# A four-layer image kernel: one tile for the exponentials' ring and delta, two PSUM banks for values, and four smaller moves between engines

## The chip, the cores and the metric

The kernel runs on one core of one Trainium2 chip. The metric is the device time of one execution in microseconds (us). A NeuronCore has five engines that run side by side: TensorE (PE, matrix products; its weight loads are listed as PEld), VectorE (DVE), ScalarE (ACT), GpSimd (POOL), and SyncE (SP), whose queue issues nearly all transfers between the chip's main memory and the on-chip memory SBUF. PE writes into PSUM[...].

## The reference

The input x is four images of 128 channels and 64 x 64 pixels in float32. Four layers follow each other, each of the form x = x + layer(group_norm(x)), with 32 groups per image. Below, n is the number of pixels, 4096.

```python
x = x + L0(gn(x))    # attention over all 4096 pixels of an image
x = x + L1(gn(x))    # 5x5 convolution, weights assembled from tables
x = x + L2(gn(x))    # two selective scans (one forward, one over the flipped pixels)
x = x + L3(gn(x))    # 3x3 convolution

# L0
q, k, v = xt @ Wq.T + bq, xt @ Wk.T + bk, xt @ Wv.T + bv      # xt: n x 128
out = softmax(q @ k.T * 128 ** -0.5) @ v

# L2, for each half of the channels (64 channels, 64 states)
xc = silu(causal_conv4(u) + conv_b); xt = xc.T
delta = softplus(xt @ Wd + bd); Bm = xt @ WB; Cm = xt @ WC
dA = exp(delta[..., None] * A); dBx = (delta * xt)[..., None] * Bm[:, :, None, :]
h[t] = dA[t] * h[t-1] + dBx[t]                                 # along the pixels
y = sum_n(h * Cm) + D * xt
```

## The kernel before

**Two streams of instructions in one order.** The program is written out by Python generators. One generator, `scan_core`, yields the ticks of the scans of all images; another, `images`, yields everything else (attention, convolution, scan operands of the images in turn, then the back ends). The driver at the end of `program` alternates them: each half tick earns a credit of `PACE / 2` (1.4), or `ENDPACE / 2` (0.75) once the ticks of the last image begin, and the other stream's steps are drawn until the credit is spent; a step yields its cost, such as `PRODUCT` (0.86), `SLOT` (0.7) or `HOP` (1.7). Each engine then executes its own instructions in the order in which they were written out. Waits between engines come from the tiles: a tile taken from a pool under a tag whose buffer is in use waits until all accesses of the tile that had the buffer are over.

**The ticks.** An image has 256 ticks, 1024 in all. A tick is 1024 pixels for 128 pairs of channel and state: POOL forms `db` (L1183, 128 x 1024), ACT the decays `da` (L1176), DVE runs the recurrence (L1193), and the result `hc` is multiplied by the rows of C either on DVE (L1196, two of 128 x 512) or on POOL (L1214, one of 128 x 1024). `to_pool(i)` decides which, at the tick's recurrence, from i mod 5: residues 0, 2 and 4 go to POOL while the set `ready` holds "operands", residues 1 and 3 otherwise; for the last image it is i mod 3 equal to 2. PE sums `hc` over the states (`collect`, L1228). The ticks of image b may start once its first operands are ready; so they run beside the attention, convolution and operands of image b+1, and those of the last image stand alone with the back ends.

**Attention.** `attention_start` normalises x in quarters and computes the values v in eight groups of 512 pixels: `keys(i)` is four products into one bank (L399), `take(i)` their eviction by ACT (L404). For images 1 to 3 it runs interleaved with the operands of the image before (`both`). `attention` then walks 256 steps: 8 blocks of 512 queries by 32 key tiles of 128. A step u computes scores (L467) into bank s or s2, ACT takes their exponential into column block u mod 8 of a ring of 8 x 512 (L473), and two steps later `values` (L479) adds the product with v. The sums of the exponentials are made by PE (`sums`, L501, four tiles at a time) or, for image 0, on DVE and POOL (`side_sums`, L521). At the end of a block `evict` copies sums and products out by ACT (zs L527, raw L529), `turn` (L541) and `invert` (L550, L552) form the reciprocals, `widen_out` (L459) spreads them, and `settle` (L564, L565) adds the block to x. In the last block all of that stood after the last values.

**Operands of the scans.** `scan_prep` normalises the image into `xn` in four pieces of 1024 pixels and stores the image; `scan_operands` works through 8 groups of 512 pixels on a table of slots: group i starts in slot 5i with the taps of the causal convolution on PE (L984; one view of xn forward, one from its end backward), `halves` on ACT (xc L998, tanh L1003), `silu` (L1007), three products (L1016), the evictions of the rows of B and C (`row`, L1021), `softplus` and `exp` on ACT, `digits` on DVE (L1035, L1036). In groups, with a switch of ACT's table, `logs` takes logarithms (L1065), `join` (L1041) adds them to delta on POOL, `drives` (L1046) multiplies delta and xc on POOL; each chunk of 1024 is stored by SP after its join (`dd`) and its drive (`dxd`). For image 0 the logarithms come in three batches (slots 20, 40 and 50), for the others in two (slots 30 and 50); joins follow one slot later, drives two slots after the joins. `delta` and the ring of the exponentials are both 128 x 4096 and take turns in the buffer "xt":

```python
ring = pools["big"].tile([P, NRING, MM], F32, tag="xt", name=f"pt_{b}")      # attention
delta = pools["big"].tile([P, L], F32, tag="xt", name=f"delta_{b}")          # scan_operands
```

The order on each engine around the change is thus fixed by the slots, the costs that are yielded, and the driver's credits.

Of the kernel before, what the change touches and what calls it, by code (L numbers as in the profile page):

```python
# [52 lines left out]
def conv_preact_kernel(  # L53
# [233 lines left out]
    def large(n, name):  # L287
        return pools["big"].tile([P, ASIZE], F32, tag=f"A{n % 2}", name=name)
    NRING = 8

# [86 lines left out]
    def attention_start(b, xn):  # L377
# [16 lines left out]
        def keys(i):  # L394

            tag = "s" if b > 0 else "saz"[i % 3]
            pvs[i] = bank(tag, f"pv_{b}_{i}").rearrange("p (t c) -> p t c", c=C)
            for t in range(TPM):
                nc.tensor.matmul(  # L399
                    pvs[i][:, t, :], xn[:, bass.ts(i * TPM + t, P)], wv, start=True, stop=True  # L400
                )
# [20 lines left out]
    def attention(b, xs, xn, v, st, safe, loads):  # L422

        ring = pools["big"].tile([P, NRING, MM], F32, tag="xt", name=f"pt_{b}")
        later = {}
# [96 lines left out]

        def evict(blk):
            zs = None
            if not fill:
                zs = pools["bg"].tile([P, MM], F32, tag="zs", bufs=1, name=f"zs_{b}_{blk}")
                nc.scalar.copy(zs, zp.pop(blk))  # L527
            raw = pools["bg"].tile([P, MM], F32, tag="raw", bufs=1, name=f"raw_{b}_{blk}")
            nc.scalar.copy(raw, acc.pop(blk))  # L529
            state[blk] = raw, zs  # L530

# [41 lines left out]
        yield HOP  # L573
        for u in range(N + 2):
            blk, j = divmod(u, NJT)
            cost = sums_due(u)
            if u < N:
                if safe and j == 0:
                    row_max(blk)
                scores(u)  # L580
                cost += PRODUCT
            w = u - 2
            if 0 <= w < N:
                values(w)
                cost += PRODUCT
                d = w % NJT
                if fill:
                    side_sums(w)
                elif d == NJT - 1:
                    sums(w)  # L590
                    cost += PRODUCT
                elif d % 4 == 3:
                    due.append((w, u + (2 if d == 3 else 1), u + NRING - 5))
                if d == NJT - 1:
                    evict(blk - 1)
                    if blk < NM:
                        for n, f in ((1, turn), (2, invert), (4, widen_out), (5, settle)):
                            after(u, n, f, blk - 1)
                    else:
                        turn(blk - 1)  # L600
                        invert(blk - 1)
                        yield PRODUCT
                        widen_out(blk - 1)
                        settle(blk - 1)
                        ready.add((b, "attended"))
                        break
            if j == 17 and blk + 1 < NM:
# [5 lines left out]
            next(loads, None)  # L613
            yield cost or HOP


# [326 lines left out]
    def scan_prep(b, xs, st, mats4):  # L943
# [8 lines left out]

        def piece(i):
            cut = slice(i * L // 4, (i + 1) * L // 4)
            normalise(xn[:, pad + cut.start : pad + cut.stop], xs[:, cut], gn)
            nc.sync.dma_start(xsd[:, cut], xs[:, cut])

        piece(0)
        piece(3)
        yield HOP  # L960
        return scan_operands(b, xn, mats4, piece)

    def scan_operands(b, xn, mats4, piece):
# [6 lines left out]
        xc = large(b, f"xc_{b}")[:, :L]  # L970
        delta = pools["big"].tile([P, L], F32, tag="xt", name=f"delta_{b}")
        pts, ths, pzs, pbs, us = {}, {}, {}, {}, {}
# [22 lines left out]
        def halves(i):  # L995

            pt = pts.pop(i)
            nc.scalar.activation(xc[:, bass.ts(i, MM)], pt, AF.Identity, scale=0.5, bias=hbias)  # L998

# [19 lines left out]
        def row(i, m):  # L1019
            bs = pools["bg"].tile([P, MM], F32, tag="w", bufs=4, name=f"bs{m}_{b}_{i}")  # L1020
            nc.scalar.copy(bs, pbs.pop((i, m)))  # L1021
            c, h = divmod(i, CH // MM)
            nc.sync.dma_start(bc[m - 1][c][:, bass.ts(h, MM)], bs)
# [14 lines left out]
        def join(c):  # L1038
            for i in range(c * CH // MM, (c + 1) * CH // MM):
                cut = bass.ts(i, MM)  # L1040
                nc.gpsimd.tensor_tensor(delta[:, cut], delta[:, cut], us.pop(i), ALU.add)  # L1041
            nc.sync.dma_start(dd[c], delta[:, bass.ts(c, CH)])
# [51 lines left out]
        for i, j in zip(cuts, cuts[1:]):  # L1094
            t = EVERY * (j - 1) + 15
            at(t, logs, i, j)
            for n, c in enumerate(range(i // PER, j // PER)):
                at(t + 1 + n, join, c)
                at(t + 3 + n, drives, c)
                at(t + 4 + n, ready.add, (b, "operands", c))  # L1100
        at(1, piece, 1)
        at(2, piece, 2)
        at(2, ready.add, (b, "read"))
        at(EVERY * (NM - 1) + 4, ready.add, (b, "taps"))
        ready.add("operands")
        for t in range(max(slots) + 1):
            for f, args in slots.get(t, ()):
                f(*args)
            yield SLOT
        ready.discard("operands")  # L1110
        ready.add((b, "all"))

# [3 lines left out]
    def scan_core(mats4, ynds, before, widen, result):  # L1116
# [11 lines left out]
        def to_pool(i):  # L1128


            if i not in pooled:
                n = i % 5
                pooled[i] = (
                    i % 3 == 2 if ticks[i][0] + 1 == B
                    else n % 2 == 0 if "operands" in ready else n % 2 == 1
                )
# [163 lines left out]
    def program(safe):  # L1300
        nonlocal more
        mats4, ynds, ends = {}, {}, {}
        ready.clear()
        if safe:
            nc.sync.dma_start(cw[:, :NKEPT, :], kept)
# [257 lines left out]
```

## Time and profile before

| | us |
|---|---|
| median of 3 runs | 4474.22 (4471.26 to 4474.52) |
| the profiled execution's own time | 4477.01 |
| its span | 4475.2 |
| PE busy | 3978.4 |
| DVE busy | 3693.8 |
| POOL busy | 3661.3 |
| ACT busy | 2401.4 |

The span runs from the first to the last instruction of the profiled execution. A row of the groups, of the timeline or of the waits names line, engine, operation and output <- inputs; in a timeline the first two numbers are start and length, xN says how many instructions were merged, and a bracket gives the engine's idle time ahead of it with the instruction that ended it. PE's products in float32 appear as two MATMUL records each. The image stages in this execution are: attention 0 until 505 us, attention 1 from about 735 to 1385, attention 2 from 1686 to 2335, attention 3 from 2641 to 3287, each followed by a convolution and the operands; the ticks begin at 687 us.

### The profile page before, as it was taken

How to read it: one execution, taken by the hardware profiler on the slowest of the kernel's cores; microseconds unless marked ns; L12 is line 12 of the kernel's file. 1: busy time of each engine (PE TensorE's matmuls, PEld its weight loads, DVE VectorE, ACT ScalarE, POOL GpSimd, SP SyncE). 2: the span in 40 equal slices, each digit the busy share in tenths (PEclk: the TensorE clock that was granted, in tenths of full speed). 3: DMA queues.
4: the chain of work that ended last, by engine and by line, in shares of the span. 5: the costliest groups of instructions: out<-in, count | busy, mean ns of one | idle time of the engine just before them, and what ended most of it. 6: DMA issues, size and time to landing. Idle time of an engine off the chain costs nothing. (4 is left out here: it accounts for less than half of the span.)

```text
span 4475.2 us, 43573 instructions
## 1 busy us (share of the span) xinstructions
PE 3978.4 (89%) x13480; PEld 1478.5 (33%) x13480; DVE 3693.8 (83%) x3663; ACT 2401.4 (54%) x4424; POOL 3661.3 (82%) x1745
## 2 busy tenths in 40 slices
PE   8999997999999979999999979999999758576766
PEld 4444443333333323333333323333333212121212
DVE  4712217999998988999999879999999799999996
ACT  3333227666665476666664566666654754544442
POOL 3433307999998979999989889999999899999995
PEclk9999999999999989999999999999999868787888
DMA  1000016545454565455545655445545666656562
GB/s 63 9 1 1 5 47 232 179 162 177 172 176 155 184 214 207 172 176 172 180 147 176 204 215 180 171 168 173 181 151 182 216 232 205 230 196 230 179 235 78
DMA packets 210002, 719.86 MB, mean 161 GB/s; under 512 B 24800, under 2 KB 25696, under 8 KB 209632
## 3 DMA queue, kind: packets, MB, share of 16 engines
q1 hardware_dynamic: 208160, 716.26, 45.8%
q8 instruction: 108, 1.77, 0.2%
q14 instruction: 134, 1.10, 0.1%
q10 hardware_dynamic: 1600, 0.73, 0.1%
HBM read 649.07 MB, written 67.83 MB: 160 GB/s over the span
## 5 line engine op out<-in xcount | busy, mean ns | idle before, releaser
L1183 POOL TENSOR_TENSOR db<-dx,br 128x1024 f32<-128x1024 f32 x1024 | 2399.5, 2366 | 214.6 <-DMA dx<-dxd 55.9
L1176 ACT ACTIVATE da<-de,a_neg 128x512 f32<-128x512 f32 (+1 forms) x1795 | 1342.0, 751 | 740.5 <-DVE da L1193 449.5
L467 PE MATMUL sc<-r,x 128*128 128x512 f32 x2048 | 1080.8, 610 | 19.0 <-ACT r L436 12.4
L479 PE MATMUL acc<-pt,v 128*128 128x512 f32 x2048 | 1046.6, 593 | 1.7
L1214 POOL TENSOR_TENSOR hc<-hc,cr 128x1024 f32<-128x1024 f32 x406 | 959.7, 2364 | 17.3 <-ACT last L1209 15.5
L473 ACT ACTIVATE pt<-sc 128x512 f32<-128x512 f32 x1024 | 604.4, 590 | 571.9 <-PE sc L467 563.3
L1228 PE MATMUL y<-hc,sel 128*32 128x512 f32 x4096 | 657.1, 653 | 275.5 <-POOL hc L1214 264.2
L1196 DVE TENSOR_TENSOR hc<-da,cr 128x512 f32<-128x512 f32 (+1 forms) x1067 | 827.7, 776 | 68.5 <-issue 0.5
L1193 DVE TENSOR_TENSOR_SCAN da<-da,last,db 128x512 f32<-128x512 f32 (+1 forms) x464 | 728.0, 1569 | 23.6 <-POOL db L1183 17.5
L1193 DVE TENSOR_TENSOR_SCAN da<-da,da,db 128x512 f32<-128x512 f32 x449 | 577.9, 1287 | 12.7 <-ACT da L1176 12.1
L467 PEld LDWEIGHTS sc<-r,x 128*128 128x128 f32 x2048 | 358.7, 189 | 604.4 <-issue 377.3
L479 PEld LDWEIGHTS acc<-pt,v 128*128 128x128 f32 x2048 | 387.5, 190 | 497.2 <-issue 478.5
L1193 DVE TENSOR_TENSOR_SCAN hc<-da,last,db 128x512 f32<-128x512 f32 (+1 forms) x304 | 455.6, 1499 | 5.8 <-POOL db L1183 2.2
L1193 DVE TENSOR_TENSOR_SCAN hc<-da,hc,db 128x512 f32<-128x512 f32 x322 | 413.1, 1283 | 55.0 <-ACT da L1176 23.3
L521 POOL TENSOR_TENSOR sidep<-sidep,pt 128x512 f32<-128x512 f32 x120 | 170.5, 1421 | 280.0 <-ACT pt L473 277.8
L1228 PEld LDWEIGHTS y<-hc,sel 128*32 128x32 f32 x4096 | 94.4, 111 | 729.0 <-POOL hc L1214 355.2
L521 DVE TENSOR_TENSOR sided<-sided,pt 128x512 f32<-128x512 f32 x120 | 96.0, 800 | 227.5 <-ACT pt L473 226.1
L904 PE MATMUL pe<-df,cw 128*128 128x512 f32 x560 | 255.2, 598 | 0.0
L1193 DVE TENSOR_TENSOR_SCAN da<-da,db 128x512 f32<-128x512 f32 (+1 forms) x154 | 231.0, 1500 | 28.1 <-ACT da L1176 15.0
L646 PE MATMUL pcm<-xpm,cw 128*128 128x512 f32 x432 | 226.0, 666 | 24.5 <-ACT xpm L372 24.5
L501 PE MATMUL zp<-pt,ones 128*32 128x512 f32 x1536 | 203.6, 595 | 5.0 <-DVE xs L565 4.9
L1209 ACT COPY last<-da 128x1 f32<-128x1 f32 x469 | 73.1, 156 | 239.5 <-DVE hc L1196 237.8
(236 smaller groups left out, 2842.4 us busy)
## 6 DMA issues: line engine op xcount, KB each, us to landing
br<-bm SPq DMA_DIRECT2D x512, 512.0 KB, 5.2
cr<-cm SPq DMA_DIRECT2D x512, 512.0 KB, 4.0
de<-dd SPq DMA_DIRECT2D x64, 512.0 KB, 4.7
dx<-dxd SPq DMA_DIRECT2D x64, 512.0 KB, 6.3
x<-in_x_dram SPq DMA_DIRECT2D x16, 512.0 KB, 5.1
xs<-in_x_dram SPq DMA_DIRECT2D x16, 512.0 KB, 5.5
xsd<-xs SPq DMA_DIRECT2D x16, 512.0 KB, 5.3
xcd<-xc SPq DMA_DIRECT2D x16, 512.0 KB, 3.3
```

The source lines that it names most:

```text
L467: nc.tensor.matmul(sc, xn[:, bass.ts(j, P)], rq[blk], start=True, stop=True)
L473: nc.scalar.activation(pt, sc, AF.Exp)
L479: nc.tensor.matmul(acc[blk], v[:, j, :], ring[:, u % NRING, :], start=j == 0, stop=j == NJT - 1)
L521: eng.tensor_tensor(s, s, ring[:, u % NRING, :], ALU.add)
L646: nc.tensor.matmul(acc.rearrange("p (r w) -> p r w", w=W), weights[:, t, :], xp[:, y : y + RPM, dx : dx + W], start=t == 0, stop=t == k * ...
L904: nc.tensor.matmul(flat(acc), cw[:, w * K5 + dx, :] if w < HSUM else more[:, w - HSUM, dx, :], view(r, dx), start=k == 1, stop=k == total ...
L1176: nc.scalar.activation(da, rep["de", b, c, d, g][:, bass.ts(h, size)], AF.Exp, scale=a_neg[:, at(i)])
L1183: nc.gpsimd.tensor_tensor(dbs[i], rep["dx", b, c, d, g], rows["b", b, c, d, q], ALU.mult)
L1193: nc.vector.tensor_tensor_scan(h, da, db[:, cut], before, ALU.mult, ALU.add)
L1196: nc.vector.tensor_tensor(hc[:, cut], h, rows["c", b, c, d, q][:, cut], ALU.mult)
L1214: nc.gpsimd.tensor_tensor(hcs[i], hcs[i], rows["c", b, c, d, q], ALU.mult)
L1228: nc.tensor.matmul(y[r : r + SG, :], sel, hcs[i - KG + 1 + gg][:, bass.ts(h, MM)], start=q == 0, stop=False, tile_position=(0, r), skip_gr ...
```

## The change

Seven things change together. (1) `exchange` gives one tile to ring and delta of all images, in place of a new one each time. (2) For images 1 to 3 the values alternate between the banks s and s2 from group 3 on. (3) `join` of the second half of the chunks goes to DVE for images 1 to 3. (4) From the slot of the last C row until the operands' end, "drives" is in `ready`, and only residue 1 of the ticks goes to POOL. (5) The normalisation of the scans' input goes in pieces of 512, from both ends to the middle; the stores stay at 1024. (6) In the last block the last four values are held back: sums come ahead of them, and `turn`, `invert` and `widen_out` are placed among them. (7) For image 0 the first half of `halves` and the rows of C are written by DVE.

```diff
+    shared = {}
+    def exchange(b):
+        if b not in shared:
+            shared[b] = shared.get(b - 1)
+            if shared[b] is None:
+                shared[b] = pools["big"].tile([P, L], F32, tag="xt", name="exchange")
+        return shared[b]
...
-            tag = "s" if b > 0 else "saz"[i % 3]
+            tag = "saz"[i % 3] if b == 0 else "s" if i < 3 else ("s", "s2")[i % 2]
...
-        ring = pools["big"].tile([P, NRING, MM], F32, tag="xt", name=f"pt_{b}")
+        ring = exchange(b).rearrange("p (r m) -> p r m", m=MM)
...
-        def evict(blk):
+        def evict_sums(blk):
             zs = None
             if not fill:
                 zs = pools["bg"].tile([P, MM], F32, tag="zs", bufs=1, name=f"zs_{b}_{blk}")
                 nc.scalar.copy(zs, zp.pop(blk))
+            state[blk] = None, zs
+
+        def evict(blk):
             raw = pools["bg"].tile([P, MM], F32, tag="raw", bufs=1, name=f"raw_{b}_{blk}")
             nc.scalar.copy(raw, acc.pop(blk))
-            state[blk] = raw, zs
+            state[blk] = raw, state[blk][1]
...
-        for u in range(N + 2):
+        HELD = 4
+        for u in range(N):
...
-            if 0 <= w < N:
-                values(w)
-                cost += PRODUCT
+            if w >= 0:
+                if w < N - HELD:
+                    values(w)
+                    cost += PRODUCT
...
                 if d == NJT - 1:
+                    evict_sums(blk - 1)
                     evict(blk - 1)
-                    if blk < NM:
-                        for n, f in ((1, turn), (2, invert), (4, widen_out), (5, settle)):
-                            after(u, n, f, blk - 1)
-                    else:
-                        turn(blk - 1)
-                        invert(blk - 1)
-                        yield PRODUCT
-                        widen_out(blk - 1)
-                        settle(blk - 1)
-                        ready.add((b, "attended"))
-                        break
+                    for n, f in ((1, turn), (2, invert), (4, widen_out), (5, settle)):
+                        after(u, n, f, blk - 1)
...
+        for w in (N - 2, N - 1) if fill else ():
+            side_sums(w)
+        blk = NM - 1
+        values(N - 4)
+        yield PRODUCT
+        while due:
+            sums(due.pop(0)[0])
+            yield PRODUCT
+        if not fill:
+            sums(N - 1)
+            yield PRODUCT
+        evict_sums(blk)
+        values(N - 3)
+        yield PRODUCT
+        turn(blk)
+        values(N - 2)
+        yield PRODUCT
+        invert(blk)
+        values(N - 1)
+        widen_out(blk)
+        evict(blk)
+        yield PRODUCT
+        settle(blk)
+        ready.add((b, "attended"))
...
-        def piece(i):
-            cut = slice(i * L // 4, (i + 1) * L // 4)
-            normalise(xn[:, pad + cut.start : pad + cut.stop], xs[:, cut], gn)
-            nc.sync.dma_start(xsd[:, cut], xs[:, cut])
+        def piece(*chunks):
+            for i in chunks:
+                cut = slice(i * MM, (i + 1) * MM)
+                normalise(xn[:, pad + cut.start : pad + cut.stop], xs[:, cut], gn)
+            for i in {i // 2 for i in chunks if i % 2}:
+                nc.sync.dma_start(xsd[:, bass.ts(i, CH)], xs[:, bass.ts(i, CH)])
 
         piece(0)
-        piece(3)
+        piece(NM - 1)
...
-        delta = pools["big"].tile([P, L], F32, tag="xt", name=f"delta_{b}")
+        delta = exchange(b)
...
-            nc.scalar.activation(xc[:, bass.ts(i, MM)], pt, AF.Identity, scale=0.5, bias=hbias)
+            if b > 0:
+                nc.scalar.activation(xc[:, bass.ts(i, MM)], pt, AF.Identity, scale=0.5, bias=hbias)
+            else:
+                nc.vector.tensor_scalar(xc[:, bass.ts(i, MM)], pt, 0.5, hbias, ALU.mult, ALU.add)
...
-            nc.scalar.copy(bs, pbs.pop((i, m)))
+            (nc.scalar.copy if m == 1 or b > 0 else nc.vector.tensor_copy)(bs, pbs.pop((i, m)))
...
-                nc.gpsimd.tensor_tensor(delta[:, cut], delta[:, cut], us.pop(i), ALU.add)
+                eng = nc.vector if b > 0 and c >= NCH // 2 else nc.gpsimd
+                eng.tensor_tensor(delta[:, cut], delta[:, cut], us.pop(i), ALU.add)
...
-        at(1, piece, 1)
-        at(2, piece, 2)
+        at(0, piece, 1, NM - 2)
+        for n in range(2, NM // 2):
+            at(n - 1, piece, n, NM - 1 - n)
...
+        at(EVERY * (NM - 1) + 13, ready.add, "drives")
...
+        ready.discard("drives")
...
                     i % 3 == 2 if ticks[i][0] + 1 == B
+                    else n == 1 if "drives" in ready
                     else n % 2 == 0 if "operands" in ready else n % 2 == 1
```

More of the change, by code (lines that the diff above doesn't have):

```diff
@@ L573, in attention @@
         yield HOP
[L574 removed]
+        HELD = 4
+        for u in range(N):
             blk, j = divmod(u, NJT)
             cost = sums_due(u)
[L577 to L580, printed above, removed]
[L581 removed]
+            if safe and j == 0:
+                row_max(blk)
+            scores(u)
+            cost += PRODUCT
             w = u - 2
[L583 to L585 removed]
+            if w >= 0:
+                if w < N - HELD:
+                    values(w)
+                    cost += PRODUCT
                 d = w % NJT
@@ L1303, in program @@
         ready.clear()
+        shared.clear()
         if safe:
```

## The prediction

> **What bounds the kernel now.** I read the page's busy shares first, then a table of windows that follows the stages, then the timelines of the windows in which TensorE (PE) is not busy.
>
> ```profile
> PE 3978.4 (89%) x13480; PEld 1478.5 (33%) x13480; DVE 3693.8 (83%) x3663; ACT 2401.4 (54%) x4424; POOL 3661.3 (82%) x1745
> ...
> PE   8999997999999979999999979999999758576766
> ...
> POOL 3433307999998979999989889999999899999995
> ```
>
> The first line is the busy time of PE and of its weight loads, of DVE and POOL; the two rows below are busy tenths in 40 slices of 112 us. The shares hide two regimes. To slice 32 PE is the full engine; after it POOL and DVE are. The windows (columns: window, length, then PE, PEld, DVE, ACT and POOL busy, PEclk, DMA share, GB/s) say it by stage:
>
> ```profile
> 630.00:750.00 120.00, 90.34 (x318) 37.10 (x317) 59.53 (x89) 82.59 (x138) 59.39 (x35) 0.90 0.56 203
> 750.00:1380.00 630.00, 623.59 (x2374) 228.49 (x2373) 594.57 (x609) 402.99 (x829) 585.53 (x253) 1.00 0.50 176
> ...
> 1575.00:1693.00 118.00, 88.46 (x336) 34.32 (x336) 88.91 (x115) 87.93 (x145) 89.84 (x49) 0.86 0.65 225
> ...
> 2530.00:2643.00 113.00, 82.27 (x318) 31.65 (x318) 86.27 (x96) 83.99 (x135) 89.44 (x46) 0.86 0.60 212
> ...
> 3476.00:3585.00 109.00, 72.47 (x260) 20.29 (x256) 86.73 (x97) 75.56 (x122) 89.88 (x46) 0.81 0.64 222
> 3585.00:4396.00 811.00, 544.71 (x1630) 154.35 (x1630) 780.78 (x458) 382.93 (x609) 774.55 (x352) 0.81 0.61 215
> ```
>
> Attention (second line) has PE at 99%: nothing taken off another engine shortens it. The last 811 us have DVE at 96% and POOL at 96%. Between images lie four handovers (scan operands of image b, values of b+1), called T01, T12, T23 and T3; in each of the first three PE idles about 30 us. There an edit can pay. PE's timeline in T12:
>
> ```profile
> 1670.03 1.16 PE L399 MATMUL pv<-wv,x 128*128 128x128 f32 x8
> 1676.86 2.08 PE L399 MATMUL pv<-wv,x 128*128 128x128 f32 x8 [5.67 <-ACT last L1209]
> 1679.61 2.08 PE L399 MATMUL pv<-wv,x 128*128 128x128 f32 x8 [0.68 <-ACT v L404]
> ...
> 1685.77 1.98 PE L467 MATMUL sc<-r,x 128*128 128x512 f32 x4 [0.84 <-ACT r L436]
> ...
> 1692.13 1.06 PE L1228 MATMUL y<-hc,sel 128*32 128x512 f32 x6 [1.02 <-POOL hc L1214]
> ```
>
> Each group of values waits for its predecessor's eviction, because all use one bank; ACT is meanwhile in logarithms and table switches. POOL in the same stretch has no gap:
>
> ```profile
> 1675.56 4.92 POOL L1041 TENSOR_TENSOR delta<-delta,u 128x512 f32<-128x512 f32 x4
> 1680.45 2.35 POOL L1183 TENSOR_TENSOR db<-dx,br 128x1024 f32<-128x1024 f32 x1
> 1682.76 4.71 POOL L1046 TENSOR_TENSOR xc<-delta,xc 128x1024 f32<-128x1024 f32 x2
> ```
>
> **What the Trainium skill says.** "PSUM — Partial Sum Buffer", Engine vs sequencer instructions: ACT, DVE and POOL take instructions strictly in order. The trace agrees: the eviction of values at 1676.22 stands behind four logarithms and two table loads of 1.28 us. "TensorE: Matmul & The Clock Gate", What's actually happening: PE halves its clock after some 3.4 us idle. It agrees: eight value matmuls take 1.16 us at 1670, 2.08 after the 5.67 us wait. "SBUF — State Buffer", Who interferes with whom: a DVE instruction with two SBUF inputs and a POOL one that reads SBUF exclude each other. It agrees: two 32-column DVE operations, 0.19 us in image 0, took 2.28 and 2.26 while POOL ran two drives:
>
> ```profile
> 2590.06 2.28 DVE L357 TENSOR_TENSOR gn_work<-gn_work 128x32 f32<-128x32 f32 x1
> 2592.38 2.26 DVE L358 TENSOR_TENSOR gn_work<-gn_work 128x32 f32<-128x32 f32 x1
> ```
>
> **The change part by part** (minus is faster).
>
> *Pieces of 512.* The first taps wait for two normalisations; two of 1024 follow each other at 1.15 us, two of 512 at 0.57. ACT's total stays (8 x 0.57 = 4.6). The forward view starts 0.57 earlier, the reversed one 1.15: I take 0.8 per image, four images: **-3.2** (0 to -4.6). SP's four stores per image stay and only change order.
>
> *Two banks for values, one shared tile.* In T12 group 6 needs eviction 4 (done 1669.6) instead of 5, so it runs at 1671. Group 7 takes its place at 1676.9, and y, the query and the scores follow: scores at about 1683 for 1685.8, **-2.7**. The first exponential of the next image waited 1.20 us for POOL's last drive, since its ring took the place of the whole delta tile. With one tile for both, only the columns that it overwrites count, and exponential u overwrites columns of chunk u/2, whose drive ended earlier: PE's 0.40 wait for the bank of that exponential goes. s2 is free for group 3: digits 6 end at 1658.7, group 3 runs at 1663.5.
>
> *Joins and share of the C products.* Two joined chunks move per image 1 to 3: POOL loses 4.92 us, DVE gains 4 x 0.69 = 2.8. They can start when the logarithms end (1671.4 to 1673.1); DVE idles 4.13 us there until 1675.28, and POOL idles until 1673.26, so three of the four meet no port conflict. The new wait is a join's for its logarithm, at DVE's head: behind it stands the scan of tick 259, which waits for its decays from ACT until 1675.28 anyhow; POOL's drives 2 and 3 and the dd stores wait for the join. Counting the residue i mod 5 along the scans, ticks 259 and 260 move from POOL to DVE (-2 x 2.36, +4 x 0.69). POOL is 9.6 us lighter, the 1.02 wait above and a 0.42 one at 1708 go. The dd and dxd stores stand before br loads on SP's queue (dxd at 1685.2, br at 1687.9) and come earlier with them. T12 in all: 2.7 + 0.4 + 1.4 = **-4.5** (-1 to -7). T23 has the same ticks (514, 515) and scores at 2641.2 that could be at 2638.6, plus a 0.23 wait: **-3** (-1 to -6).
>
> *T01.* Joins stay on POOL. Ticks 4 and 5 leave it, 6 joins it: net one product less. Scores can come at 731.5 instead of 735.6 (group 7 behind eviction 5 at 727.2); POOL, unbroken from 728 to 755, gains 2.4. *C rows and halves of image 0* take 8 x 0.48 + 8 x 0.57 = 8.4 us off ACT and put 16 x 0.69 on DVE (row L1036, one PSUM operand; ACT's 0.58 is the other bound). Early on the loop is copy, product, 16 taps (3.66), product, so the slower copy loses 0.1 a turn; from 696 to 722 ACT is full and 1.5 us less of it helps the evictions. T01: **-3.5** (0 to -6).
>
> *Last values follow sums.* In images 1, 2 and 3 PE waited 0.91, 0.70 + 0.56 and 0.70 + 0.56 = 3.4 us around turn and widen_out; two values now lie in each wait: turn, at PE's head, waits for the copy zs on ACT, and a value (0.86 us) runs before it; widen_out waits for the reciprocal on DVE, and two run before that. The copy raw comes later, beside widen_out (1.0 us against 0.58). In image 0 turn would wait 0.5 us for POOL's last side sum instead of 0.6 for the inversion: nothing. More shares are yielded, so up to one more tick (4 us of DVE) can stand ahead of settle, for which the convolution waits 8 to 9 us. **-3** (+3 to -4).
>
> *T3.* Tick 766 goes to POOL and 767 to DVE: even. The joins meet a full POOL (3560 to 3582), and DVE is the bound after it. Unhindered they fit DVE's idle 3.03 us at 3564. If each waits for a POOL instruction, 4 x (2.36 + 0.69) = 12.2, less 3.0 idle and what POOL wins: **+2** (-2 to +7).
>
> Sum: -3.2 - 4.5 - 3 - 3.5 - 3 + 2 = **-15.2**. The profiled execution took 4477.0 us (span 4475.2, 1.8 around it) and would take 4461.8; it is 2.8 above the median of the runs, so the forecast is 4474.2 - 15.2 = **4459**.
>
> **The rivals.**
> *B, the handovers are bound elsewhere.* ACT is full from 1650 to 1677 with work that no edit removes for images 1 to 3, and PE goes cold anyway; or dependencies stay those of the whole tile. Pieces and tails remain: -3.2 - 3 + 2 = 4470. Against it: the waits at 1679.6 and 1692.1 have nothing to do with ACT's logarithms.
> *C, PE stays warm.* Keys, y and query at half clock cost 3.4 us in T12; with the outer ends of the three handovers (-19 instead of -11), pieces (-4.6), tails (-4) and T3 at -2: -29.6, 4444.6. Against it: the 5.67 us wait only shrinks to about 4.6, above 3.4.
> *A, slower: the shared port.* If POOL wins the port between any two joins, each of 12 costs 3.05 us: 36.6, less DVE's idle 4.1 + 4.1 + 3.0 = 25 lost. The -7.5 of T12 and T23 go too; -9.7 stays (pieces, T01, tails): 4489. It decides as soon as POOL has work queued when the logarithms end; T3 shows that, T12 and T23 show POOL idle.
>
> **How the numbers follow.** Forecast 0.55, B 0.20, C 0.17, A 0.08. A measurement here tells about 0.2%, 8.9 us, from no change: faster is below 4465.3, slower above 4483.1. Faster: 0.52 + 0.04 + 0.17 = 0.73. Same: 0.03 + 0.15 + 0.03 = 0.21. Slower: 0.01 + 0.05 = 0.06. The range 4438 to 4474 holds C with some 6 us beyond its outer ends and B up to no change at all (its own sum with tails and pieces at nothing); A is left out.
>
> **What would show it.** Right: the wait before values group 6 falls below 1 us and moves to group 7; the first exponential waits no longer for L1046; joins L1041 on DVE near 0.7 us; POOL's gapless stretch after T12 is some 9 us shorter; PE's waits for zs and zr are gone. Wrong: joins of 2 us and more (A); scores less than 1 us earlier relative to the logarithms (B); tails longer because settle stands behind a tick.

## The result and the profile after

The kernel after took 4472.07 us in the median of 12 runs (4469.3 to 4476.42), the kernel before 4473.14 beside it (12 runs); the ratio is 0.9998, with an interval of 0.9989 to 1.0006. Timed again later with the experiments it was 4471.6, ratio 0.9994 (0.9986 to 1.0003). The forecast was 4459, so the expected 15 us didn't come. The profiled execution took 4469.3 us, that of before 4477.0, so the two traces lie 7.7 us apart where the medians lie 1 to 2 apart. The traced run of after was the fastest of its twelve, and that of before was 4 us above its median. Single traces are therefore used to see what waits for what, and medians for what an edit is worth.

The windows of the stages (window, length, then PE, PEld, DVE, ACT and POOL busy, PEclk, which is the clock granted to PE as a share of full speed, DMA share, GB/s):

```profile
630.00:750.00 120.00, 90.59 (x310) 36.77 (x308) 70.48 (x107) 74.47 (x124) 53.51 (x32) 0.89 0.56 203
...
1575.00:1693.00 118.00, 89.41 (x344) 31.70 (x340) 96.18 (x123) 89.05 (x149) 87.13 (x46) 0.87 0.69 250
2530.00:2643.00 113.00, 89.45 (x350) 33.32 (x351) 96.27 (x112) 90.53 (x151) 88.77 (x43) 0.88 0.71 246
3476.00:3585.00 109.00, 79.31 (x272) 21.09 (x272) 88.62 (x88) 75.73 (x126) 88.43 (x41) 0.80 0.69 245
3585.00:4396.00 811.00, 549.80 (x1629) 152.96 (x1628) 782.78 (x458) 382.64 (x606) 773.05 (x352) 0.80 0.59 210
```

The work went where it was sent. In the first window ACT has 8.1 us less (82.6 before) and DVE 11.0 more; in T12 (second line) and T23 DVE has 7.3 and 10.0 more, POOL 2.7 and 0.7 less. Yet PE's busy time in T12 is only 1 us up (88.5 before). DVE, the engine with 29 us to spare in T12, now has 22. PE's timeline in T12 shows why that did not help:

```profile
1671.40 1.16 PE L411 MATMUL pv<-wv,x 128*128 128x128 f32 x8 [1.34 <-ACT v L416]
1677.42 2.08 PE L411 MATMUL pv<-wv,x 128*128 128x128 f32 x8 [4.86 <-ACT last L1253]
1679.43 1.65 PE L1272 MATMUL y<-hc,sel 128*32 128x512 f32 x8
1683.69 1.74 PE L446 MATMUL pr<-x,wqk 128*128 128x512 f32 x2 [2.62 <-ACT last L1253]
1686.21 5.15 PE L479 MATMUL sc<-r,x 128*128 128x512 f32 x6 [0.78 <-ACT r L448]
```

Values group 6 comes at 1671.4 for 1676.9 before, group 7 takes the long wait, y comes 2.2 us earlier: all as forecast. Then the query waits 2.62 us, and the scores stand at 1686.2, where they stood at 1685.8. The last eviction is late because ACT takes its instructions in order and waits 4.29 us for the scans on DVE to free a buffer of decays, and these scans stand behind the four joins. DVE first, then ACT, then POOL, same stretch:

```profile
1673.32 5.94 DVE L1081 TENSOR_TENSOR exchange<-exchange,u 128x512 f32<-128x512 f32 x4 [1.05 <-ACT u L1105]
1679.18 1.22 DVE L1237 TENSOR_TENSOR_SCAN da<-da,db 128x512 f32<-128x512 f32 x1
```

```profile
1677.45 0.69 ACT L1220 ACTIVATE da<-de,a_neg 128x512 f32<-128x512 f32 x1
1682.43 0.69 ACT L1220 ACTIVATE da<-de,a_neg 128x512 f32<-128x512 f32 x1 [4.29 <-DVE da L1237]
1683.06 0.58 ACT L416 COPY v<-pv 128x512 f32<-128x512 f32 x1
1683.54 0.16 ACT L1253 COPY last<-da 128x1 f32<-128x1 f32 x1
1683.73 0.69 ACT L1220 ACTIVATE da<-de,a_neg 128x512 f32<-128x512 f32 x1
1684.36 0.58 ACT L416 COPY v<-pv 128x512 f32<-128x512 f32 x1
```

```profile
1672.37 2.34 POOL L1227 TENSOR_TENSOR db<-dx,br 128x1024 f32<-128x1024 f32 x1
1675.94 2.77 POOL L1086 TENSOR_TENSOR xc<-exchange,xc 128x1024 f32<-128x1024 f32 x1 [1.23 <-DVE exchange L1081]
1679.39 2.41 POOL L1086 TENSOR_TENSOR xc<-exchange,xc 128x1024 f32<-128x1024 f32 x1 [0.68 <-DVE exchange L1081]
```

The four joins take 5.94 us instead of 2.8: POOL has a `db` running when they begin and a drive when they end. In "SBUF — State Buffer", Who interferes with whom, the Trainium skill says that an operation of DVE with two SBUF inputs and one of POOL that reads SBUF contend for a shared port, and that this port is an exclusive lock. The trace agrees from both sides: two of the joins took 1.94 and 2.87 us where the other two took 0.68, and the first drive took 2.77 us where the second took 2.41.

In T01 the halves on DVE hold ACT up. ACT, then DVE:

```profile
698.34 0.68 ACT L1220 ACTIVATE da<-de,a_neg 128x512 f32<-128x512 f32 x1
703.67 0.69 ACT L1040 ACTIVATE th<-pt,hbias 128x512 f32<-128x512 f32 x1 [4.65 <-issue]
704.25 1.23 ACT L384 ACTIVATE x<-x,nb_a,rs_a 128x1024 f32<-128x1024 f32 x1
```

```profile
699.80 0.68 DVE L1059 COPY bs<-pb 128x512 f32<-128x512 f32 x1
700.41 1.21 DVE L1237 TENSOR_TENSOR_SCAN hc<-da,db 128x512 f32<-128x512 f32 x1
701.65 1.28 DVE L1237 TENSOR_TENSOR_SCAN hc<-da,hc,db 128x512 f32<-128x512 f32 x1
702.85 0.73 DVE L1035 TENSOR_SCALAR xc<-pt,hbias 128x512 f32<-128x512 f32 x1
```

The trace names no releaser for the 4.65 us of idle ACT ("issue"), but the tanh L1040 begins 0.09 us after DVE's xc L1035 ends, and for the groups before it the trace names this xc as the releaser (2.67 to 3.68 us of idle ACT each). Both read one PSUM bank (a tile of 128 x 512 float32 in this program), and the xc was written out first. It stands behind a row copy and the two scans of a tick; behind the tanh on ACT stands the normalisation that the first values product needs. That product runs at 705.5 instead of 699.2.

At the end of attention 1 the inversion stands behind scans that were let in (DVE, then PE; `turn` had ended at 1381.15):

```profile
1385.44 0.69 DVE L1240 TENSOR_TENSOR hc<-da,cr 128x512 f32<-128x512 f32 x1
1386.05 0.15 DVE L565 COPY zall<-pz 128x4 f32<-128x4 f32 x1
```

```profile
1383.04 1.12 PE L491 MATMUL acc<-exchange,v 128*128 128x512 f32 x2
1386.56 1.55 PE L471 MATMUL pzb<-ident,zr 128*128 128x128 f32 x8 [2.39 <-DVE zr L567]
```

### The profile page after: what moved, and what is told of

Same layout as the page of the kernel before. It is cut to its first block, busy times and chain, and to the rows that moved or that the text cites. A ratio compares the mean times of both kernels' runs of the same rounds, so it can differ in the third digit from the quotient of the medians.

```text
span 4467.5 us, 43584 instructions
## 1 busy us (share of the span) xinstructions
PE 3980.8 (89%) x13480; PEld 1470.8 (33%) x13480; DVE 3726.3 (83%) x3703; ACT 2399.7 (54%) x4425; POOL 3638.1 (81%) x1728
## 5 line engine op out<-in xcount | busy, mean ns | idle before, releaser
L491 PE MATMUL acc<-exchange,v 128*128 128x512 f32 x2048 | 1048.4, 594 | 1.7
L1258 POOL TENSOR_TENSOR hc<-hc,cr 128x1024 f32<-128x1024 f32 x401 | 947.7, 2363 | 19.3 <-ACT last L1253 16.5
L485 ACT ACTIVATE exchange<-sc 128x512 f32<-128x512 f32 x1024 | 604.7, 591 | 590.5 <-PE sc L479 583.8
L1237 DVE TENSOR_TENSOR_SCAN da<-da,da,db 128x512 f32<-128x512 f32 x455 | 585.7, 1287 | 22.6 <-ACT da L1220 21.8
L491 PEld LDWEIGHTS acc<-exchange,v 128*128 128x128 f32 x2048 | 387.0, 190 | 496.7 <-issue 478.4
L1237 DVE TENSOR_TENSOR_SCAN hc<-da,hc,db 128x512 f32<-128x512 f32 x317 | 406.7, 1283 | 41.4 <-ACT da L1220 11.4
L533 POOL TENSOR_TENSOR sidep<-sidep,exchange 128x512 f32<-128x512 f32 x120 | 170.5, 1421 | 279.1 <-ACT exchange L485 276.9
L533 DVE TENSOR_TENSOR sided<-sided,exchange 128x512 f32<-128x512 f32 x120 | 96.1, 801 | 227.4 <-ACT exchange L485 226.1
L513 PE MATMUL zp<-exchange,ones 128*32 128x512 f32 x1536 | 201.6, 596 | 8.0 <-DVE xs L580 7.9
```

The costliest lines, as they stand in the source:

```text
L485: nc.scalar.activation(pt, sc, AF.Exp)
L491: nc.tensor.matmul(acc[blk], v[:, j, :], ring[:, u % NRING, :], start=j == 0, stop=j == NJT - 1)
L533: eng.tensor_tensor(s, s, ring[:, u % NRING, :], ALU.add)
L1237: nc.vector.tensor_tensor_scan(h, da, db[:, cut], before, ALU.mult, ALU.add)
L1258: nc.gpsimd.tensor_tensor(hcs[i], hcs[i], rows["c", b, c, d, q], ALU.mult)
```

## The experiments

All of them were timed beside the kernel before; 0.001 of the time is 4.5 us. A table of stages from their traces follows at the end. First, **one edit undone at a time.** Halves and C rows back on ACT:

```diff
-            if b > 0:
-                nc.scalar.activation(xc[:, bass.ts(i, MM)], pt, AF.Identity, scale=0.5, bias=hbias)
-            else:
-                nc.vector.tensor_scalar(xc[:, bass.ts(i, MM)], pt, 0.5, hbias, ALU.mult, ALU.add)
+            nc.scalar.activation(xc[:, bass.ts(i, MM)], pt, AF.Identity, scale=0.5, bias=hbias)
...
-            (nc.scalar.copy if m == 1 or b > 0 else nc.vector.tensor_copy)(bs, pbs.pop((i, m)))
+            nc.scalar.copy(bs, pbs.pop((i, m)))
```

> The kernel after, with the halves and the C rows of image 0 back on ScalarE. Theory 1 (an edit's loss ate another's gain: here the halves on VectorE, for whose xc ScalarE's tanh waits 2.7 to 3.7 us a group): no tanh of image 0 waits for VectorE; the last taps of image 0 end about 2.5 us earlier than in the kernel after (696.5), the first values product of image 1 runs at about 699 instead of 705.5, the first scores of image 1 at 734 or earlier instead of 738.5; the time is 1 to 3 us less than after's, 4469 to 4471. Theory 2 (the handover of image 0 is bound elsewhere, by the logarithms and the joins): the first values move by 6 us all the same, but the first scores of image 1 move by less than 1 us and the time does not change.

Measured: 4463.2, ratio 0.9977 (0.9968 to 0.9986). The first values product of image 1 ran at 699.7, its scores at 732.9, as theory 1 had it. The edit was a loss. It is larger than expected, 9 us against after's median for 6 us seen in T01; where the other 3 come from, these traces can't say.

Joins back on POOL:

```diff
-                eng = nc.vector if b > 0 and c >= NCH // 2 else nc.gpsimd
-                eng.tensor_tensor(delta[:, cut], delta[:, cut], us.pop(i), ALU.add)
+                nc.gpsimd.tensor_tensor(delta[:, cut], delta[:, cut], us.pop(i), ALU.add)
```

> The kernel after, with the joins of the second half back on GpSimd (the share of C products that moved to VectorE stays). Theory 1 (the joins on VectorE wait for the port: 5.9 us for four in the handover from image 1 to 2, and 9.4 us in the last one, where 2.8 was forecast): the scan of tick 259 runs near 1675.5 instead of 1679.2, the last values eviction of image 2 at 1680 to 1682 instead of 1684.4 and the first scores of image 2 at 1682 to 1684 instead of 1686.2; in the last handover VectorE gains 6 to 9 us and GpSimd has 5 more; the time is 0 to 6 us less than after's 4472. Theory 2 (GpSimd was the bound there, as the forecast had it, and joins on VectorE are a gain even blocked): the drives of chunks 2 and 3 come 5 to 6 us later again, y and the first scores of image 2 come 1 to 3 us later than in the kernel after, and the time is 2 to 5 us more, 4474 to 4477.

Measured: 4459.4, ratio 0.9968 (0.9956 to 0.9980), 12 to 13 us below after, twice the most that was expected. The last eviction of image 2 came at 1680, its scores at 1684.0; the drives came 3 to 4 us later, and that cost less. The first scores of image 3 came 8.5 us earlier than in the kernel after, of which 6.3 were lost again in the first block of queries, where PE waited 3.9 us for POOL's hc. Theory 2, that GpSimd needs the relief even at that price, falls.

The old end of attention (the new loop and its tail taken out, the old ones of the diff put back):

> The kernel after, with the end of an image's attention as it was before (all values in their turn, then both copies, turn, inversion, spread). Theory 1 (the new tail saves nothing, since the inversion stands behind a tick's scans on VectorE in one case and the settle does in the other): last scores to last settle is again 6.7, 10.3, 8.2 and 8.9 us for images 0 to 3 (after: 8.8, 11.3, 9.6, 12.2, of which 0.9 is only the order of the scores), the convolutions start within 1 us of where they start in the kernel after relative to the last scores, and the time is within 2 us of 4472. Theory 2 (the forecast: a wait of 1 us per image is gone): the time is 3 us more, 4475.

Measured: 4465.1, ratio 0.9986 (0.9979 to 0.9992). From last scores to last settle it took 6.6, 10.3, 7.7 and 9.8 us, close to what theory 1 expected, but neither theory had the time: the new tail was no gain but a loss. Its size is uncertain, 4 to 5 us by the ratios, whose intervals overlap, and 7 by the medians; the tails themselves differ by 4.0 us (34.4 for 42.0 less 3.6, see the table).

Now **edits alone.** The kernel before with the shared tile and the two banks:

> The kernel before with two of the edits alone: one tile for the exponentials' ring and delta, and two banks for the values. Theory 1 (these two work, and what hides them in the kernel after is the joins on VectorE): the wait before values group 6 of images 2 and 3 falls under 1.5 us, the first scores of image 2 come at 1683 to 1684 instead of 1685.8, those of image 3 come 2 us earlier relative to those of image 2, the first exponential waits no longer for GpSimd's drive, and the time is 3 to 6 us less than before's 4473, 4467 to 4470. Theory 2 (GpSimd's gapless stretch is the bound of the handover, so that values that come earlier only wait longer for y): the first scores move by less than 1 us and the time stays 4472 to 4474.

Measured: 4473.1, ratio 1.0002 (0.9994 to 1.0011). The first scores of image 2 came at 1683.0, as theory 1 had it, and the time is that of theory 2. What took the gain is PE's wait for POOL's hc after the first scores of images 1, 2 and 3 (total us, times, longest):

```profile
PE y L1238 <- POOL hc L1224: 4.6, 1, 4.6
PE y L1238 <- POOL hc L1224: 3.7, 1, 3.7
PE y L1238 <- POOL hc L1224: 6.4, 2, 3.6
```

In the kernel before these waits are 1.0, 1.4 and 0.2 us, so they grew from 2.6 to 14.7. The tile and the banks were not tried apart. With the pieces of 512 added (same edits, and `piece` of the diff):

> As the last one, but GpSimd's share of C products as in the kernel before: the kernel before with one tile for ring and delta, two banks for values and pieces of 512. It tells what the smaller share is worth. Theory 1 (pieces of 512 are worth the 3 us forecast, 0.8 per image, and the smaller share frees GpSimd for the drives): 4469 to 4471 here, since tile and banks alone gave 1.0002, and the rest of what the last kernel gains is the share's. Theory 2 (the gain is the pieces', the share does nothing because GpSimd's products only move to VectorE): within 3 us of the last kernel.

Measured: 4473.4, ratio 0.9999 (0.9991 to 1.0008). Neither theory holds for the time: it is not 2 to 4 us below the kernel before, and it is 13 us above the next kernel. In the trace the pieces do what they should: after POOL's last operation of the statistics (nb_s) the first taps start 0.43 us sooner in each of the four images, and the eighth record of the taps 0.72 us sooner. PE in T12 of this kernel:

```profile
1680.98 2.94 PE L477 MATMUL sc<-r,x 128*128 128x512 f32 x6 [0.84 <-ACT r L446]
1683.75 1.02 PE L489 MATMUL acc<-exchange,v 128*128 128x512 f32 x2
1684.71 1.04 PE L1241 MATMUL y<-hc,sel 128*32 128x512 f32 x2
1689.91 1.93 PE L1241 MATMUL y<-hc,sel 128*32 128x512 f32 x6 [4.16 <-POOL hc L1227]
1691.76 1.83 PE L477 MATMUL sc<-r,x 128*128 128x512 f32 x2
```

Scores start early, do six records, and then y stands at PE's head for 4.16 us waiting for POOL; the two records of scores after it take 1.83 us, where two take 1.02 later. In the kernel before that wait was 1.02.

With the share of C products as well, that is the kernel after without halves, joins and tail:

> The kernel after without three of its edits: halves and C rows of image 0 back on ScalarE, joins back on GpSimd, the end of an image's attention as before. What stays: one tile for ring and delta, two banks for values, pieces of 512, the smaller GpSimd share of C products while drives are due. Theory 1 (the three are separate losses that add up: measured one by one against after's 0.9998 they cost 0.0021, 0.0030 and 0.0012 of the time, 28 us together): ratio to the kernel before 0.9935, about 4444 us. Theory 2 (they overlap, since a handover that is freed of one is bound by the next, and without one of them half of the other's loss is gone): 0.9960 to 0.9970, 4455 to 4460, no better than after without the joins alone (0.9968).

Measured: 4460.5, ratio 0.9969 (0.9957 to 0.9982). Theory 2 holds: three undone together are worth no more than the joins undone alone. Against the run before it the share is worth 0.0030, and PE's waits for hc in the three first blocks fall from 11.6 to 4.2 us. The share alone, on the kernel before:

```diff
+        at(EVERY * (NM - 1) + 13, ready.add, "drives")
...
+        ready.discard("drives")
...
+                    else n == 1 if "drives" in ready
                     else n % 2 == 0 if "operands" in ready else n % 2 == 1
```

> The kernel before with one edit alone: while drives are due, GpSimd takes one C product in five of the last ticks before an image's operands are done, rather than three. Theory 1 (this edit is the whole gain of the kernel with four edits, 0.9969, since tile, banks and pieces without it gave 0.9999): ratio 0.9965 to 0.9978, GpSimd's drives 2 and 3 of image 1 end some 2 to 5 us earlier than in the kernel before. Theory 2 (tile and banks bring the scores earlier, and the share makes room for it; each alone is worth nothing): ratio 0.9990 to 1.0005.

Measured: 4465.9, ratio 0.9983 (0.9976 to 0.9989), between the two theories: more than half of that kernel's gain is this edit's, and PE's waits for POOL's hc in the first blocks, 2.6 us in the kernel before, are gone from the trace. The rest, 0.0014, is not clear: the two intervals overlap.

**Mends.** The tanh first, the halving by DVE second:

```diff
-            else:
-                nc.vector.tensor_scalar(xc[:, bass.ts(i, MM)], pt, 0.5, hbias, ALU.mult, ALU.add)
...
             nc.scalar.activation(ths[i], pt, AF.Tanh, scale=0.5, bias=hbias)
+            if b == 0:
+                nc.vector.tensor_scalar(xc[:, bass.ts(i, MM)], pt, 0.5, hbias, ALU.mult, ALU.add)
```

> The kernel after with one change of order in image 0: ScalarE's tanh reads the taps' bank first and VectorE's halving second. Theory 1 (the halves on VectorE cost because ScalarE's tanh waits for VectorE, which is in scans, statistics and digits; VectorE has the time itself): ScalarE waits for no xc, the tanh of group 7 runs near 699 instead of 703.7, the first values product of image 1 at 700 to 701 instead of 705.5, and the time is 5 to 10 us less than after's, ratio 0.9976 to 0.9987, as with the halves on ScalarE. Theory 2 (it is VectorE's load, the halves being late whoever reads first, since silu and the products wait for them): first values product of image 1 later than 704 and the time within 2 us of after's.

Measured: 4462.6, ratio 0.9975 (0.9965 to 0.9986). On ACT:

```profile
695.31 0.69 ACT L1038 ACTIVATE th<-pt,hbias 128x512 f32<-128x512 f32 x1 [0.53 <-DMA bm<-bs]
695.90 1.23 ACT L384 ACTIVATE x<-x,nb_a,rs_a 128x1024 f32<-128x1024 f32 x1
```

The tanh of group 7 runs 8.4 us earlier, the first values product at 698.0, which is 1.7 us ahead of the kernel with the halves on ACT. So DVE had the time for halves and C rows; it was the order of the two reads. Theory 2 falls.

The tail without its two points for ticks:

```diff
         evict_sums(blk)
         values(N - 3)
-        yield PRODUCT
         turn(blk)
         values(N - 2)
-        yield PRODUCT
         invert(blk)
```

> The kernel after with its new end of attention, but without the two points between the copy of the sums and the inversion at which a tick of the scan may be issued (sums copy, values, turn, values, inversion, values, spread, then the copy of raw follow each other on their queues). Theory 1 (the new order is good, and it is the ticks let in that stand before the inversion and the settle on VectorE, 2.0 to 5.9 us): the inversion runs within 0.5 us of the turn's end in images 1 to 3, last scores to last settle falls from 11.3, 9.6 and 12.2 to about 9, 8 and 8.5 us, and the time is 4 to 8 us less than after's, ratio 0.998 to 0.999. Theory 2 (the order itself costs: raw is copied late, after the last values): the tails stay within 1 us of after's and the time within 2 us.

Measured: 4462.9, ratio 0.9973 (0.9963 to 0.9984). Last scores to last settle fell to 7.1, 9.2 and 9.3 us in images 1 to 3. The inversion ran 1.0 us after the turn's end in image 1 (4.9 in the kernel after) and 0.04 in image 3 (2.85). PE:

```profile
1380.31 0.95 PE L556 MATMUL pz<-zsel,zs 128*128 128x1 f32 x8
1381.12 1.96 PE L491 MATMUL acc<-exchange,v 128*128 128x512 f32 x4
1382.92 1.05 PE L471 MATMUL pzb<-ident,zr 128*128 128x128 f32 x8
```

No wait is left in it: the new order is good, and the ticks were the loss, so theory 1 has the mechanism. But 9 us by the medians is more than the 7.4 us of the tails, part of which can come back where the ticks run instead. The joins are shorter too, since they now fall elsewhere among the ticks; T12 is 3.8 us shorter, yet T01 and T23 are 2.1 and 2.3 longer, so the traces do not show what this is worth. The group of the twelve joins on DVE, kernel after and this one (columns: ns shortest/median/longest, first and last start):

```profile
L1081 DVE TENSOR_TENSOR exchange<-exchange,u x12: 679/2256/2871, 1673.3 to 3568.4; 128x512 f32<-128x512 f32 x12
```

```profile
L1079 DVE TENSOR_TENSOR exchange<-exchange,u x12: 678/684/2884, 1667.5 to 3554.7; 128x512 f32<-128x512 f32 x12
```

In the kernel after most joins are blocked, 23.2 us for the twelve; here the median join is free, 13.8 us. With the old tail they took 19.0.

As a control the kernel after once more:

> The kernel after, unchanged, timed and profiled a second time, as a control for the others: five variants of it that each undo or mend one thing came out 0.0012 to 0.0030 below the kernel before, and all three undone together no lower. Theory 1 (the kernel after loses what it gains, and is really 10 us slower than any of its mended variants, which are then bound by one and the same thing): ratio 0.9990 to 1.0005, 4470 to 4475. Theory 2 (its first figure was a bad draw): ratio 0.9975 to 0.9985, 4462 to 4467, and most single losses are about nothing.

Measured: 4471.6, ratio 0.9994 (0.9986 to 1.0003): theory 1. The three mends together (tanh first, no ticks in the tail, joins on POOL), and the same with the joins left on DVE:

> The kernel after with the three mends together: tanh ahead of the halves in image 0, no tick between the sums' copy and the inversion at the end of attention, joins on GpSimd. Theory 1 (mends don't add: what is left in the handovers is GpSimd's backlog and the scans' own work): 4456 to 4461, ratio 0.9960 to 0.9972, like the joins alone. Theory 2 (they add: 0.0023 + 0.0025 + 0.0030 below after): ratio 0.9920 to 0.9940, 4437 to 4446, faster than both kernels by over 0.5%.

> The kernel after with two mends alone: tanh ahead of the halves, no tick between the sums' copy and the inversion. The joins of the second half stay on VectorE. With the first of these mends alone the twelve joins took 23.0 us, with the second alone 13.8, unhindered they take 8.2. Theory 1 (joins on VectorE cost what GpSimd's queue makes them wait, so where the earlier end of attention lets them meet an idle GpSimd they cost nothing): the twelve take under 16 us and the ratio is that of the kernel with all three mends, 0.9949, within 0.001. Theory 2 (the joins are a loss for VectorE's order whether blocked or not, since the scan of the next tick stands behind them): ratio 0.9960 to 0.9975, 4456 to 4463, and the joins take 13 to 24 us.

Measured: 4451.9, ratio 0.9949 (0.9935 to 0.9963), and 4453.5, ratio 0.9956 (0.9942 to 0.9969). The first lies between its two theories: the mends add to a good part, but not fully (singly 0.0021 + 0.0023 + 0.0028 = 0.0072 below after's 0.9996, the mean of its two ratios; together 0.0047). It beats both kernels, by 22 us the kernel before. In the second the twelve joins on DVE took 13.3 us, and its ratio is within 0.001 of the first's, so theory 1 is favoured: joins that meet an idle POOL cost little. But each interval reaches about 0.0014 to either side, so a small loss is not ruled out.

The stages, us, from single traces (the two of after show the scatter; a traced run lies up to 5 us from its kernel's median). Handovers run from first taps to first scores; tails are last scores to last settle, summed over four images, of which about 0.9 each in all rows with the new tail is only the place of the last scores. "First block" is the time from the first record of scores to the 65th, that is 32 scores or one block of queries; the column after it runs from the last logarithm to the last large operation on DVE:

| kernel | T01 | T12 | T23 | tails | first block, images 1 to 3 | last logarithm to end | joins on DVE |
|---|---|---|---|---|---|---|---|
| before | 91.0 | 99.4 | 106.3 | 34.0 | 77.5, 78.9, 76.0 | 902.3 | |
| tile and banks | 87.9 | 96.1 | 99.6 | 35.2 | 80.9, 81.1, 83.9 | 899.9 | |
| tile, banks, pieces, share | 87.7 | 96.4 | 99.7 | 34.4 | 76.2, 78.2, 79.2 | 902.1 | |
| share only | 91.9 | 99.4 | 106.8 | 34.1 | 73.7, 75.1, 77.0 | 898.6 | |
| after | 93.6 | 100.3 | 100.5 | 42.0 | 75.6, 75.9, 74.1 | 899.1 | 23.2 |
| after again | 93.7 | 100.4 | 102.6 | 41.5 | 76.3, 75.5, 74.1 | 898.3 | 23.3 |
| halves undone | 87.6 | 101.6 | 101.0 | 41.4 | 76.0, 76.6, 74.6 | 899.5 | 22.6 |
| tanh first | 86.5 | 101.3 | 101.0 | 42.2 | 76.0, 75.6, 74.2 | 897.8 | 23.0 |
| joins undone | 95.6 | 98.3 | 95.4 | 41.7 | 77.5, 75.4, 80.4 | 895.1 | |
| tail undone | 95.3 | 96.5 | 100.9 | 34.4 | 75.8, 78.2, 76.5 | 902.2 | 19.0 |
| tail mended | 95.7 | 96.5 | 102.8 | 34.6 | 75.9, 75.4, 76.7 | 900.3 | 13.8 |
| all three mended | 86.2 | 96.2 | 99.5 | 32.9 | 77.3, 75.9, 76.4 | 900.6 | |
| tanh and tail mended | 86.3 | 95.9 | 102.5 | 32.9 | 75.5, 75.2, 76.2 | 900.4 | 13.3 |

Two differences in these traces do not come from the edits' own work. T01 is about 2 us longer in the kernels with the joins undone, the tail undone and the tail mended than in the kernel after, though undoing the joins changes nothing before T12. Taps of one group in image 0, the kernel after, then that with the joins undone:

```profile
679.87 3.66 PE L1018 MATMUL pt<-xn,wtap 128*64 128x512 f32 x16
```

```profile
679.40 5.35 PE L1018 MATMUL pt<-xn,wtap 128*64 128x512 f32 x16
```

The clock granted to PE from 676 to 690 us was 0.88 in these three kernels and 1.00 in all others. And after the last instruction on DVE the span runs on for 9.0 to 9.9 us in the kernel after (both traces), with the halves undone and with the tanh first, but for 6.8 to 7.3 us in all others, before included. So 2 to 3 us between after and the kernels with another tail or with the joins on POOL lie behind the last computation; the traces name no cause.

## Why the prediction was right or wrong

The range held the result at its upper part, but the likeliest case, faster by 15 us, did not come, and that the number stayed inside is luck: gains and losses that the forecast did not have cancelled. In the two traces the handovers are 2.3 us shorter in sum, the first blocks 6.8 and the stretch after the last logarithm 3.2; the tails are 4.4 us longer, and the end behind the last instruction 2.2. By its steps:

**Two banks and one tile: right in place, wrong in worth.** The forecast gave -2.7, -0.4 and most of -3 and -3.5. The second row of the table shows T01, T12 and T23 shorter by 3.1 + 3.3 + 6.7 = 13.1 us; the first blocks after them are longer by 3.4 + 2.2 + 7.9 = 13.5, of which 12.1 are PE's longer waits for POOL's hc, and the time does not change. The step that failed is "y, the query and the scores follow". The forecast had shown that POOL has no gap in that stretch, yet counted the start of the scores as the gain, while the next y must still wait for POOL's backlog. Scores that start earlier only reach that wait earlier. "Nothing taken off another engine shortens" an attention was read from a window that begins at 750 us, behind the first scores (735.6) and the first wait for hc.

**Share of the C products: right in kind, sized too small.** "POOL relief" was 1.4 us in T12 and 2.4 in T01. Alone it gave 0.0017, 7.6 us, where tile and banks alone gave nothing; the first blocks of images 1 and 2 are 3.8 us shorter each (that of image 3 is 1.0 longer), and no wait for hc is left in them. So the queue that bounds the start of an attention is POOL's, and that step should have led the sum.

**Joins on DVE: the step that failed is "three of the four meet no port conflict".** It read POOL as idle from the trace of before, in which POOL stood idle at that moment. In the kernel after the other edits had moved that moment. Four joins took 6.2, 7.5 and 9.6 us in the three images, not 2.8. That "the scan of tick 259 waits anyhow until 1675.28" did not hold either: it ran at 1679.18, and ACT's eviction behind it. Rival A had the mechanism right, and its point of decision too ("as soon as POOL has work queued when the logarithms end"), but not its size: 23.2 us for twelve joins, where it had 36.6. For T3 +2 was forecast, and its sign stays open: the stretch after the last logarithm is 3 to 4 us shorter in after than in before, another 3 to 4 shorter with the joins undone, and the same with and without them (900.4 and 900.6) once the other two mends are in.

**Halves and C rows of image 0: wrong in sign.** The term said that the slower copy loses 0.1 a turn and that 1.5 us less ACT helps later. It costed the load, 8.4 us off ACT, rightly (8.1 in the window), and left out a wait that the edit adds: the tanh, at ACT's head, waits for an instruction behind scans on DVE. T01 was to be 3.5 us shorter and was 2.6 longer; without this edit it is 3.4 shorter (87.6), so the rest of the term alone gave what the whole had promised.

**Tails: right in order, wrong in what stands between.** Forecast -3, with +3 as the outer end "up to one more tick can stand ahead of settle". Less the 0.9 per image, the tails were some 4 us longer; in images 1 and 3 the ticks stood ahead of the inversion, not of settle alone. With the two points taken out they are 34.6 - 3.6 = 31.0 us, the forecast 3 shorter than before's 34.0.

**Pieces of 512: right.** Between 0.43 (first taps) and 0.72 us (eighth record) per image, 1.7 to 2.9 in four, forecast 3.2; the total does not show it.

**Rival B** said 4470, the nearest number, but for another reason: ACT's logarithms. Undoing single edits frees some 4 to 13 us with the logarithms left as they are. Why the losses add so little is shown in part. Joins and tail overlap through the place of the joins among the ticks, as the last column shows. The 2 to 3 us at the end of the span are counted both in the joins' loss and in the tail's, and the lower clock in T01 lengthens three of the variants. What is left of the gap between 0.0072 and 0.0047 stays open.

## What to carry to other kernels

An earlier start is a gain only up to the next queue that has a backlog: look for the first instruction behind the new start that waits for the fullest engine, and price that. Before work is moved to an engine with time to spare, ask which instruction of the old engine will wait for it, and write the reader that no one waits for last. Before a stage is compared between two single traces, look at the granted clock, and at stages that the edit cannot touch. A gap seen in one trace belongs to that timing; an edit whose worth depends on meeting it should be costed at its blocked price as soon as other edits move the same stretch.

## What was not expected of the hardware

The lock between DVE and POOL does not strike each operation alike. Among the joins of one batch some took 0.68 us and others 2.82 to 2.87, longer by about one operation of POOL (2.35); in T12 of the kernel after the four took 1.94, 0.68, 0.68 and 2.87. A small operation was hit too: the `fit` of 128 x 128 (L1537), 0.20 us in the kernel before, took 1.73 in the kernel after, in the middle of the last tail, while POOL ran a product of 2.34 us. That it was this lock is read from the overlap alone.

In this program two reads of one PSUM bank by two engines follow each other: in image 0's groups the tanh began 0.03 to 0.10 us after DVE's xc had ended (652.14 after 652.10, 703.67 after 703.58). Whether the bank itself would allow both at once was not tried.
